# Position-dependent 7x7 attention: the two logits layers on four 64x64 parts of the array, positions as a matmul, one maximum call, filled three-tap slots

## The chip, the core and the metric

The kernel runs on one core of a Trainium2 chip. The time is that of one execution of the whole program on the device, in microseconds (us); the times below are medians over runs. The profile is one execution taken by the hardware profiler. Engine names are those of the profile: PE (matmul), PEld (its weight load), DVE (VectorE), ACT (ScalarE), POOL (GpSimd), SP (SyncE, which issues most DMAs here).

## The reference, cut to what matters

The program has two layers on a tensor of 4 images, 256 channels, 56x56. The change lies in the first. After a group norm, three 1x1 convolutions give `x1` and `x2` (32 channels) and `x3` (256 channels). For each of the 49 taps of a 7x7 window (borders reflected):

```python
sub2 = x1[:, :, None] - unfold_patches(x2)            # 32 channels
subp = p[:, :, None] - unfold_patches(p)              # 2 channels, positions only, the same for every image
y = relu(bn_eval(concat([sub2, subp])))               # 34 channels x 49 taps x 3136 places
y = relu(bn_eval(conv1x1(y, cw1)))                    # 34 -> 32   ("hidden")
wgt = softmax(conv1x1(y, cw2, cb2), axis=taps)        # 32 -> 32   ("logits")
out[:, :, s] = sum over taps of patch(x3)[:, :, s] * wgt[tap]    # 32 weights, each for 8 channels s
```

The second layer (attention with squared scores, a router that picks half of the tokens, a feed-forward on those) is not touched.

## The kernel before

**Tiling.** All is float32. An image is cut into 14 blocks of 4 rows (`RB`), 224 places each; 4 images give 56 blocks. The 128 partitions hold 4 taps x 32 channels. The 49 taps make 13 slots (`SLOTS`, L77): ten of 4 taps, and three, slots 10 to 12, of 3 taps, which use 96 partitions (`size`). A slot's patch is a shifted view into a ring of rows in SBUF, `ac` for `x2` and `xc` for `x3`, whose four partition groups were loaded with shifts of 0 to 3 columns; `aw` and `xw` serve the slots whose taps are neighbours downwards.

**A block's work.** `relation` (L488): `differ` subtracts on POOL into `y1`, `bend` does the first ReLU on ACT, `hidden` is the first matmul with `cw1`, a 128x128 matrix with four 32x32 blocks on its diagonal, `bend_more` the second ReLU on ACT (out of PSUM into `y2`), `logits` the matmul with `cw2`, of the same form, and `keep` copies the logits with their bias to `lg` on ACT. These four go by pairs of slots: a matmul of 400 columns (50 inner columns of 4 rows, 2 slots) for `hidden`, 448 for `logits`. `softmax` (L611) takes the maximum over slots on DVE, then over the four taps within the partitions by two matmuls with a rotation matrix (`turn`), subtracts, exponentiates, and sums. `values` (L690): 8 of the 13 products with `x3` on DVE (1792 elements each, weights copied to PSUM by `weights` first), 5 on POOL, and `add` sums each product over its taps into PSUM by four matmuls of 32 columns of the array (`same`), which run side by side.

**Positions.** What the two position channels add to `hidden` is the same for all inner columns of an inner block. `positions` (L247) works it out once; the inner columns get it as the bias `tb` of `bend_more`, one ACT instruction for each slot. The 3 columns at each side go a way of their own: `borders` (a matmul of 240 and one of 72 columns), `place_borders` (DVE, adds `near`), `bend_borders` (ACT). In the first and the last block of an image `load_pos` fetches the positions by DMA on ACT's queue, and `hidden` adds them by a second matmul for each pair of slots.

**Beside it.** `planes` (L298) makes `x1`, `x2`, `x3` of a following image in chunks of 8 rows, one chunk for each block, as 12 passes of 448 columns; its `x3` is taken out of PSUM by DVE. `statistics` makes the group norm's sums of an image, `ready` the layer norm of finished chunks of image 0, one in every second block's time from the eighth to the twentieth.

**Order.** Each engine's instructions stand in the order of the program (`InOrder`). The loop (L809) goes over steps, 14 (`ROUND`) for a block; `AT` (L94) gives each part its step and its rank within the step, counted from a block's own start. Blocks overlap: a block's `hidden` runs some 30 steps ahead of its products. Matmul outputs of `relation`, `planes`, `statistics` and `ready` share the PSUM pool `mm`: 4 buffers of one bank. Products share `prod`, 4 buffers in SBUF; a product takes the buffer that was given back first.

Of the kernel before, what the change touches and what calls it, by code (L numbers as in the profile page):

```python
# [7 lines left out]
F32 = mybir.dt.float32  # L8
# [7 lines left out]
P = 128  # L16
# [5 lines left out]
PAD = 3  # L22
# [24 lines left out]
    + ["b1", "b2", "cb2", "b3_0", "b3_1", "q_0", "q_1", "k_0", "k_1", "v_0", "v_1", "pb_0", "pb_1"]  # L47
# [11 lines left out]
def bn_affine(nc, pool, par, n, eps, tag):  # L59
# [12 lines left out]

ROW, COLUMN = 0, 1
# [10 lines left out]
HALVES = [(0, 10), (10, 13)]  # L84
INNER = W - 2 * PAD
# [9 lines left out]
    "load_relation": (-12, 4), "load_first": (23, 4), "load_values": (32, 5), "differ": (-5, 6),  # L95
    "bend": (-2, 9), "load_pos": (-1, 7), "hidden": (4, 5), "borders_0": (1, 5),
    "place_borders_0": (3, 9), "bend_borders_0": (6, 9), "borders_1": (3, 5),
    "place_borders_1": (7, 0), "bend_borders_1": (14, 3), "bend_more": (5, 5), "logits": (7, 1),
    "keep": (8, 7), "begin": (22, 1), "largest_0": (23, 3), "largest_1": (25, 6), "split": (27, 0),
    "join": (27, 7), "turned_0": (28, 7), "over_0": (29, 1), "turned_1": (29, 4), "over_1": (30, 1),  # L100
    "lower_0": (30, 1), "exp_0": (31, 0), "lower_1": (32, 5), "exp_1": (32, 8), "lower_2": (31, 9),
    "exp_2": (33, 0), "add_up_0": (33, 4), "add_up_1": (33, 5), "gather": (34, 1),
    "spread": (34, 1), "invert": (36, 1), "weights": (31, 5), "ours": (33, 0), "add_ours": (34, 0),
    "pools": (33, 6), "add_pools": (36, 9), "divide": (47, 1), "more": (51, 7), "store": (55, 3),
# [6 lines left out]
def conv_layer(ctx: ExitStack, tc: tile.TileContext, d, xs: bass.AP, ln0: bass.AP):  # L111
# [16 lines left out]
    bordersd = dram.tile([8, NS, 3 * FB4], F32, name="bordersd")  # L128
    insided = dram.tile([8, NS], F32, name="insided")
# [4 lines left out]
    )  # L134
    whole_image = lambda a, n: a[n].rearrange("(c p) f -> p c f", p=P)
# [21 lines left out]
    cw1p = const.tile([8, P], F32, name="cw1p")  # L157
# [3 lines left out]
    turn = const.tile([P, 2, P], F32, name="turn")  # L161
    nc.scalar.dma_start(turn, d["turn"])
# [18 lines left out]
    mm = ctx.enter_context(tc.tile_pool(name="mm", bufs=4, space=PSUM))  # L181
# [12 lines left out]
    def statistics(n):  # L194
# [13 lines left out]
        pm = mm.tile([P, 512], F32, tag="mm", name=f"pm{n}")  # L208
        te.matmul(pm[:, 0:2], gavg, mv[:, :, 0], start=True, stop=True)
# [7 lines left out]
        pv = mm.tile([P, 512], F32, tag="mm", name=f"pv{n}")  # L217
        te.matmul(pv[:, 0:2], gavg, dv, start=True, stop=True)
# [14 lines left out]

    tb = const.tile([P, NS], F32, name="tb")
    near = const.tile([P, 3, NS * RB * 2 * PAD], F32, name="near")
# [9 lines left out]
    def positions():  # L247

        pl = pp.tile([8 * NS, 2, 3 * FB4], F32, name="pl")
        ve.tensor_scalar(pl, loc[:, 0], pposs[:, 4:5], None, ALU.mult)  # L250
        yield
        ve.scalar_tensor_tensor(pl, loc[:, 1], pposs[:, 5:6], pl, ALU.mult, ALU.add)
        yield
        ve.tensor_scalar(pl, pl, pposs[:, 6:7], None, ALU.add)
        cen = pp.tile([8 * NS, 3 * FB4], F32, name="cen")
        ve.tensor_tensor(cen, pl[:, 0], pl[:, 1], ALU.subtract)
        yield
        se.activation(cen, cen, AF.Relu, bias=tp1, scale=sp1)
        inside = pp.tile([8 * NS, 1], F32, name="inside")
        ve.tensor_copy(inside, cen[:, FB4 + W // 2 : FB4 + W // 2 + 1])  # L260
        less = pp.tile([8 * NS, 3 * FB4], F32, name="less")
        ve.tensor_scalar(less, cen, inside, None, ALU.subtract)
        for j in range(2):
            r = slice(j * 4 * NS, (j + 1) * 4 * NS)
            nc.sync.dma_start(insided.rearrange("(g j) t -> j t g", j=2)[j], inside[r])
            nc.scalar.dma_start(bordersd.rearrange("(g j) t f -> j t g f", j=2)[j], cen[r])
            nc.sync.dma_start(posd.rearrange("(g j) t f -> j t g f", j=2)[j], less[r])
        at8 = pp.tile([8, NS], F32, name="at8")
        nc.sync.dma_start(at8, insided)
        edge = pp.tile([8, 3, NS, RB, 2, PAD], F32, name="edge")  # L270
        for b in range(3):
            for i in range(2):
                at = b * FB4 + i * (W - PAD)
                src = bordersd[:, :, at : at + 1]
                nc.scalar.dma_start(
                    edge[:, b, :, :, i],
                    bass.AP(
                        src.tensor, src.offset,
                        [list(src.ap[0]), list(src.ap[1]), [W, RB], [1, PAD]],
                    ),  # L280
                )
        for _ in range(10):
            yield
        pt = mm.tile([P, 512], F32, tag="mm", name="pinside")
        te.matmul(pt[:, :NS], cw1p, at8, start=True, stop=True)
        ve.tensor_scalar(tb, pt[:, :NS], s2, t2, ALU.mult, ALU.add)
        n = NS * RB * 2 * PAD
        for b in range(3):
            pt = mm.tile([P, 512], F32, tag="mm", name=f"pnear{b}")
            te.matmul(  # L290
                pt[:, :n], cw1p, edge[:, b].rearrange("p t h i w -> p (t h i w)"),
                start=True, stop=True,
            )
            ve.tensor_scalar(near[:, b], pt[:, :n], s2, t2, ALU.mult, ALU.add)
# [3 lines left out]
    def planes(n, q):  # L298
# [13 lines left out]
        pt = mm.tile([P, 512], F32, tag="mm", name=f"p12_{at}")  # L312
        for c in range(2):
            te.matmul(pt[: 2 * REL, :CH], w12[:, c], t[:, c], start=c == 0, stop=c == 1)
# [15 lines left out]
        for g in range(2):  # L330
            pt = mm.tile([P, 512], F32, tag="mm", name=f"p3_{at}_{g}")
            for c in range(2):
                te.matmul(
# [4 lines left out]
            ve.tensor_scalar(  # L338
                stag[:, g, own, PAD : PAD + W],
                pt[:, :CH].rearrange("p (h w) -> p h w", w=W),  # L340
                col(f"b3_{g}"), None, ALU.add,
# [40 lines left out]
    prod = ctx.enter_context(tc.tile_pool(name="prod", bufs=4))  # L382
# [10 lines left out]
    y1s = [yp.tile([P, NS, FB4], F32, name=f"y1_{i}", bufs=1) for i in range(2)]  # L393
    y2 = yp.tile([P, NS, FB4], F32, name="y2", bufs=1)
    xc = x3p.tile([P, SH, RING, WP], F32, name="xc", bufs=1)
    ac = ap.tile([P, 1, RING, WP], F32, name="ac", bufs=1)

# [38 lines left out]
    def patch(k, ring, w, t, which):  # L436
# [5 lines left out]
        return a[: taps * REL, which, r : r + RB, kj : kj + W]  # L442
# [34 lines left out]
    size = lambda t: SLOTS[t][3] * REL  # L477
    pairs = [(t, min(t + 2, NS)) for t in range(0, NS, 2)]

    def inner(y, t, e, pn):  # L480

        return view(y[:pn], t * FB4 + PAD, [[W, (e - t) * RB], [1, INNER]])

    def outer(y, t, e, pn):

        return view(y[:pn], t * FB4, [[W, (e - t) * RB], [W - PAD, 2], [1, PAD]])

    def relation(k):  # L488

        aw, a1 = held.pop(("a", k))  # L490
        border = {0: 0, H // RB - 1: 2}.get(blocks[k][1])
        y1 = y1s[k % 2]
        p1s, p2s = {}, {}

        def differ(i):

            a, z = GROUPS[i]
            m, pn = z - a, size(a)
# [3 lines left out]
                y1[:pn, a:z].rearrange("p t (h w) -> p t h w", w=W),  # L502
                a1[:pn].unsqueeze(1).to_broadcast([pn, m, RB, W]),
# [7 lines left out]
        def bend(i):  # L511
            a, z = GROUPS[i]
            se.activation(y1[: size(a), a:z], y1[: size(a), a:z], AF.Relu)

        def hidden(t, e):
            p1 = p1s[t] = mm.tile([P, 512], F32, tag="mm", name=f"p1_{k}_{t}")
            n = (e - t) * RB * INNER
            te.matmul(
                p1[:, :n], cw1[: size(t)], inner(y1, t, e, size(t)),
                start=True, stop=border is None, skip_group_check=True,  # L520
            )
            if border is not None:
                te.matmul(
                    p1[:, :n], cw1p, inner(held.pop(("pos", k, t)), 0, e - t, 8),
                    start=False, stop=True, skip_group_check=True,
                )

        def borders(i):

            t, e = HALVES[i]  # L530
            p1 = p1s["borders", i] = mm.tile([P, 512], F32, tag="mm", name=f"pb_{k}_{i}")
            te.matmul(
                p1[:, : (e - t) * RB * 2 * PAD], cw1[: size(t)], outer(y1, t, e, size(t)),
                start=True, stop=True,
            )

        def place_borders(i):

            t, e = HALVES[i]
            n = RB * 2 * PAD  # L540
            pn = size(t)
            be = p1s["placed", i] = yp.tile(
                [P, HALVES[0][1] * n], F32, tag="be", name=f"be_{k}_{i}", bufs=2
            )
            ve.scalar_tensor_tensor(
                be[:pn, : (e - t) * n], p1s.pop(("borders", i))[:pn, : (e - t) * n], s2[:pn],
                near[:pn, 1 if border is None else border, t * n : e * n],
                ALU.mult, ALU.add,
            )
# [1258 lines left out]
```

## Time and profile before

| | us |
|---|---|
| median of 3 runs (3821.7 to 3825.9) | 3825.31 |
| the profiled execution's own time | 3829.45 |
| its span | 3827.1 |
| first subtraction on POOL (`y<-a,ac`) | 76.4 |
| first `o<-acc,rz` (a block's end on DVE) | 172.2 |
| last `o<-acc,rz` | 1864.4 |

The first layer fills the span up to 1864 us, the second one the rest. Busy over the whole span: PE 91%, DVE 66%, ACT 52%, POOL 51%; the granted clock of PE was 0.954 on average and 1.00 in most blocks of the first layer. The `o<-acc,rz` rows, one for each block, cut the first layer into blocks, so that the distance of two of them is what one block costs. Of the 55 distances, 17 are 25.8 to 26.0 us, 15 are 30.4, four are 35.0, three are 27.4 to 27.8; ten lie between 31.0 and 38.8 around the end of an image, five between 36.3 and 56.8 where the statistics of an image are made, and the last is 17.1. Blocks of 30.4 have a chunk of `planes` in them, those of 35.0 also one of `ready`.

### The profile page before, as it was taken

The numbers are of one execution on the slowest core, as the hardware profiler recorded it, in microseconds if no ns is written. First come the engines' busy times: TensorE is split into PE (matmuls) and PEld (weight loads), VectorE is DVE, ScalarE is ACT, GpSimd is POOL, SyncE is SP. The second block draws the span as 40 slices with busy tenths as digits, with TensorE's granted clock in tenths as the row PEclk, the third lists the DMA queues.
The fourth block names the chain that finished last, engine by engine and source line by source line (L and its number), as shares of the span: only waits on it lengthen the run. The fifth ranks groups of instructions, "written<-read, shape, count | busy, mean of one in ns | idle before, by whom it ended". The sixth has DMA issues, their size and how long they took to land. (4 is left out here: it accounts for less than half of the span.)

```text
span 3827.1 us, 77232 instructions
## 1 busy us (share of the span) xinstructions
PE 3464.3 (91%) x30654; PEld 1469.0 (38%) x30654; DVE 2512.9 (66%) x3475; ACT 1991.4 (52%) x4181; POOL 1937.2 (51%) x1165
## 2 busy tenths in 40 slices
PE   3989998999979998999799989898899989889999
PEld 1333333333323333333243334333433344335666
DVE  2688888889778988999773457444754475434211
ACT  2767766777557765776235533444345424442111
POOL 1568887789768887998650026022512142110321
PEclk7999999999989999999899899998999999899999
DMA  3756656665566646655302210132012200231110
GB/s 97 161 134 145 138 133 157 141 136 105 131 143 141 138 91 136 128 117 108 99 2 50 57 46 7 41 83 60 10 29 73 64 19 12 60 93 40 55 51 27
DMA packets 328007, 330.99 MB, mean 86 GB/s; under 512 B 68651, under 2 KB 315407, under 8 KB 327647
## 3 DMA queue, kind: packets, MB, share of 16 engines
q1 hardware_dynamic: 309509, 289.68, 33.6%
q0 software_dynamic: 11408, 32.32, 2.7%
q10 hardware_dynamic: 6730, 4.05, 0.5%
q8 instruction: 241, 3.95, 0.4%
q14 instruction: 119, 0.97, 0.1%
HBM read 256.78 MB, written 68.68 MB: 85 GB/s over the span
## 5 line engine op out<-in xcount | busy, mean ns | idle before, releaser
L858 POOL TENSOR_TENSOR pr<-xc,lg 128x1792 f32<-128x1792 f32 x280 | 1034.9, 3705 | 279.0 <-ACT lg L858 102.2
L858 PE MATMUL acc<-pr,same 128*32 128x448 f32 (+1 forms) x5824 | 678.0, 558 | 71.0 <-DVE pr L858 57.0
L858 PE MATMUL p<-y,cw 128*128 128x400 f32 (+5 forms) x1568 | 681.9, 539 | 2.4 <-ACT y L858 1.5
L858 DVE TENSOR_TENSOR pr<-xc,exp 128x1792 f32<-128x1792 f32 x280 | 559.6, 1999 | 53.9 <-DMA xc<-x3d 30.2
L858 ACT ACTIVATE ph<-pg,unit 128x896 f32<-128x896 f32 x448 | 426.2, 1000 | 250.3 <-PE pg L858 249.5
L858 ACT ACTIVATE y<-p,tb,bn2s 128x200 f32<-128x200 f32 (+1 forms) x728 | 341.8, 519 | 226.3 <-PE p L858 222.1
L858 PEld LDWEIGHTS p<-y,cw 128*128 128x128 f32 (+1 forms) x1568 | 266.2, 191 | 399.7 <-issue 202.4
L858 POOL TENSOR_TENSOR phi<-ls 128x512 f32<-128x512 f32 (+1 forms) x200 | 242.9, 1215 | 264.0 <-PE accs L858 155.9
L858 DVE TENSOR_TENSOR phi<-pv,ls 128x1408 f32<-128x1408 f32 (+1 forms) x200 | 322.0, 1619 | 67.4 <-PE accs L858 48.6
L858 DVE TENSOR_TENSOR pr<-xw,exp 128x1792 f32<-128x1792 f32 x168 | 338.5, 2016 | 41.2 <-issue 16.0
L858 POOL DMA_DIRECT2D out<-tk x28 | 20.9, 746 | 647.9 <-ACT tk L858 599.5
L858 PE MATMUL pg<-qT,pairs 32*128 32x448 f32 x1792 | 303.9, 610 | 46.4 <-ACT ph L858 46.3
L858 POOL TENSOR_TENSOR y<-a,ac 128x896 f32<-128x896 f32 x168 | 277.7, 1654 | 126.7 <-DMA ac<-x3d 95.7
L858 PEld LDWEIGHTS acc<-pr,same 128*32 128x32 f32 (+1 forms) x5824 | 144.4, 110 | 429.9 <-issue 247.2
L858 POOL DMA_INDIRECT us<-rows,to x112 | 107.6, 961 | 320.7 <-DMA us<-rows,to 223.8
L858 ACT ACTIVATE ls<-pv 128x256 f32<-128x256 f32 (+1 forms) x200 | 77.3, 386 | 366.1 <-PE pv L858 333.7
L858 PE MATMUL accs<-phi,v 128*32 128x512 f32 (+1 forms) x1600 | 219.8, 613 | 38.2 <-POOL phi L858 27.9
L858 PE MATMUL pv<-wqkv,xn 128*32 128x256 f32 x3136 | 215.8, 390 | 42.4 <-DVE phi L858 22.7
L858 ACT ACTIVATE lg<-p,par 128x448 f32<-128x448 f32 x392 | 233.1, 595 | 4.6 <-PE p L858 4.6
L858 PE MATMUL acc<-ph,cf 128*32 128x448 f32 (+1 forms) x1792 | 229.8, 586 | 0.0
L858 ACT ACTIVATE lg<-lg 128x1120 f32<-128x1120 f32 x168 | 163.9, 1007 | 97.3 <-DVE lg L858 96.8
L858 DVE COPY av<-acc 128x448 f32<-128x448 f32 x56 | 35.0, 625 | 272.2 <-PE acc L858 272.1
(256 smaller groups left out, 5276.9 us busy)
## 6 DMA issues: line engine op xcount, KB each, us to landing
xw<-x3d SPq DMA_DIRECT2D x224, 248.0 KB
xq<-in_x SPq DMA_DIRECT2D x47, 448.0 KB
xc<-x3d SPq DMA_DIRECT2D x54, 248.0 KB
xc<-x3d SPq DMA_DIRECT2D x54, 247.0 KB
xc<-x3d SPq DMA_DIRECT2D x54, 246.0 KB
xc<-x3d SPq DMA_DIRECT2D x54, 245.0 KB
xr<-in_x SPq DMA_DIRECT2D x224, 56.0 KB
xs<-xr SPq DMA_DIRECT2D x224, 56.0 KB
```

The source lines that it names most:

```text
L858: return lambda *a, **k: self.tc.keep_in_program_order(of(*a, **k))
```

## The change

- `hidden` and `logits` use the array as four parts of 64 rows by 64 columns. `cw1` has nothing outside its diagonal blocks, so its upper left 64x64 serves taps 0 and 1 and its lower right 64x64 taps 2 and 3. Four slots make a batch (`BATCHES`, 3 of four slots and one of slot 12 alone): four matmuls of 448 columns, one for each part of the array, go to `p1[slot pair, tap half]`, and the tap halves lie in two PSUM banks. `logits` turns this back.
- Positions: `pos`, a constant tile of 13 slots, is a second set of four matmuls in every batch of every block (`cw1p`). It is reloaded by SP, batch by batch, where the next block's kind (first, inner, last of an image) differs. `tb`, `near`, `borders` and what belongs to them are gone.
- `bend_more` is one ACT instruction of 128x896 for a batch, `keep` one of 128x896, or two of 128x448 in the batch where slots 10 and 11 have 3 taps.
- The three slots of 3 taps get a fourth whose logit is -1e30 (`cb2_3`), so that all instructions have 128 partitions; the columns of the rings that this tap reads are set to 0 once.
- The maximum over slots is one `tensor_reduce` over 13 x 224 elements; that over taps is two transposes, a `tensor_reduce`, and eight matmuls of 32 columns of the array.
- `weights` copies two slots at a time. `planes` takes `x3` out of PSUM on ACT instead of DVE. The other matmuls of the layer are cut into quarters of 32 columns of the array (`by_quarters`).
- `mm` has 2 buffers of two banks, `prod` 5 buffers, `y1` one buffer instead of two. `AT` is new; `load_relation` moves from step -12 to -8, against a first `differ` at step -4 instead of -5.

```diff
-    mm = ctx.enter_context(tc.tile_pool(name="mm", bufs=4, space=PSUM))
+    mm = ctx.enter_context(tc.tile_pool(name="mm", bufs=2, space=PSUM))
...
+    matmul = lambda out, lhsT, rhs, start, stop: by_quarters(te, out, lhsT, rhs, start, stop)
...
-            ve.tensor_scalar(
+            se.activation(
                 stag[:, g, own, PAD : PAD + W],
                 pt[:, :CH].rearrange("p (h w) -> p h w", w=W),
-                col(f"b3_{g}"), None, ALU.add,
+                AF.Identity, bias=col(f"b3_{g}"),
             )
...
+    def batch(a, q, j):
+        if q < BATCHES - 1:
+            return a[:, 4 * q + 2 * j : 4 * q + 2 * j + 2]
+        return a[:, NS - 1, j * (FB4 // 2) : (j + 1) * (FB4 // 2)]
+    halves = [slice(i * HALF_P, (i + 1) * HALF_P) for i in range(2)]
+    width = lambda q: 2 * FB4 if q < BATCHES - 1 else FB4 // 2
...
-        def hidden(t, e):
-            p1 = p1s[t] = mm.tile([P, 512], F32, tag="mm", name=f"p1_{k}_{t}")
-            n = (e - t) * RB * INNER
-            te.matmul(
-                p1[:, :n], cw1[: size(t)], inner(y1, t, e, size(t)),
-                start=True, stop=border is None, skip_group_check=True,
-            )
+        def hidden(q):
+            n = width(q)
+            p1 = p1s[q] = mm.tile([P, 2, 512], F32, tag="mm", name=f"p1_{k}_{q}")
+            for w, of in ((cw1, y1), (cw1p, pos)):
+                for i, taps in enumerate(halves):
+                    for j, to in enumerate(halves):
+                        te.matmul(
+                            p1[to, i, :n], w[taps, taps], batch(of, q, j)[taps],
+                            start=of is y1, stop=of is pos, skip_group_check=True,
+                        )
+            if after != kind:
+                load_pos(4 * q, min(4 * q + 4, NS), after, sy)
...
-        def bend_more(t, e):
-            p1 = p1s.pop(t)
-            n = RB * INNER
-            for a in range(t, e):
-                pn = size(a)
-                se.activation(
-                    inner(y2, a, a + 1, pn),
-                    p1[:pn, (a - t) * n : (a - t + 1) * n].rearrange("p (h w) -> p h w", w=INNER),
-                    AF.Relu, bias=tb[:pn, a : a + 1], scale=s2[:pn],
-                )
+        def bend_more(q):
+            n = width(q)
+            y2 = y2s[q] = yp.tile([P, 2, 2 * FB4], F32, tag="y2", name=f"y2_{k}_{q}")
+            se.activation(y2[:, :, :n], p1s.pop(q)[:, :, :n], AF.Relu, bias=t2, scale=s2)
+        def logits(q):
+            n = width(q)
+            p2 = p2s[q] = mm.tile([P, 2, 512], F32, tag="mm", name=f"p2_{k}_{q}")
+            y2 = y2s.pop(q)
+            for j, part in enumerate(halves):
+                for i, taps in enumerate(halves):
+                    te.matmul(
+                        p2[taps, j, :n], cw2[part, part], y2[part, i, :n],
+                        start=True, stop=True, skip_group_check=True,
+                    )
...
-        def begin():
-            se.activation(z[:, :, :FB4], lg[:, 0:2], AF.Identity)
-        def largest(*parts):
-            for t, i, n in parts:
-                m = z[: size(t), i : i + n, :FB4]
-                ve.tensor_tensor(m, lg[: size(t), t : t + n], m, ALU.max)
...
+        def largest():
+            ve.tensor_reduce(mx, lg.rearrange("p t f -> p f t"), AX.X, ALU.max)
+        def turned():
+            for i in range(2):
+                te.transpose(
+                    z[:TB, 0, i * P : (i + 1) * P], mx[:, i * TB : (i + 1) * TB], ident
+                )
+        def over_turned():
+            ve.tensor_reduce(
+                most, z[:TB, 0, :].rearrange("p (i g c) -> p i c g", i=2, g=4), AX.X, ALU.max
+            )
+        def turned_back():
+            for i in range(2):
+                for j in range(4):
+                    te.matmul(
+                        z[j * REL : (j + 1) * REL, 1, i * TB : (i + 1) * TB], most[:, i],
+                        ident[:TB, :TB], start=True, stop=True, skip_group_check=True,
+                    )
```

## The prediction

> **What bounds the kernel now.** I read the granted clock first (1.00 in the blocks below), then the busy time by windows that run from one `o` row to the next, one block each, then the groups by shape inside five plain blocks (1634.64 to 1764.26 us), then the timeline of PE for what one pass costs. Windows (length, then busy us of PE, PEld, DVE, ACT, POOL; clock; DMA):
>
> ```profile
> 897.54:923.44 25.90, 25.84 (x170) 9.83 (x168) 25.63 (x25) 18.95 (x41) 25.73 (x11) 1.00 0.52 109
> 652.32:682.73 30.41, 30.41 (x181) 11.63 (x181) 27.08 (x28) 24.24 (x63) 26.49 (x11) 1.00 0.64 152
> 682.73:717.69 34.96, 33.62 (x189) 13.03 (x189) 31.14 (x34) 27.35 (x62) 27.23 (x12) 1.00 0.63 137
> 949.34:981.09 31.75, 31.75 (x178) 11.24 (x170) 25.89 (x26) 18.95 (x41) 25.13 (x11) 1.00 0.60 119
> ```
>
> A plain block (first line) has three engines full at once: PE, DVE and POOL. With `planes` (second) or position matmuls (fourth) PE alone is full; with `ready` too (third) PE has 33.62 of 34.96. So less work on PE and DVE helps wherever a block is longer than 25.9, and POOL, whose work stays, holds a plain block where it is.
>
> Groups in the five plain blocks:
>
> ```profile
> L858 POOL TENSOR_TENSOR pr<-xc,lg 128x1792 f32<-128x1792 f32 x16 | 59.2, 3716 | 0.7 <-ACT lg L858 0.6
> L858 POOL TENSOR_TENSOR y<-a,ac 128x896 f32<-128x896 f32 x5 | 9.8, 1962 | 0.0
> L858 DVE TENSOR_TENSOR z<-lg,z 128x448 f32<-128x448 f32 x20 | 12.5, 623 | 0.3
> L858 ACT ACTIVATE y<-p,tb,bn2s 128x200 f32<-128x200 f32 x51 | 23.7, 518 | 13.7 <-PE p L858 13.6
> ```
>
> The timeline of PE (start, us), in the first layer and in the second:
>
> ```profile
> 1025.41 0.96 PE L858 MATMUL acc<-pr,same 128*32 128x448 f32 x8
> 1026.30 1.73 PE L858 MATMUL p<-y,cw 128*128 128x400 f32 x4
> 1027.96 1.71 PE L858 MATMUL acc<-pr,same 128*32 128x448 f32 x16
> 1029.60 1.73 PE L858 MATMUL p<-y,cw 128*128 128x400 f32 x4
> ...
> 2173.80 0.94 PE L858 MATMUL pu<-qT,gram 128*32 128x448 f32 x8
> 2174.66 1.03 PE L858 MATMUL pg<-qT,pairs 32*128 32x448 f32 x8
> 2175.62 0.96 PE L858 MATMUL acc<-ph,cf 128*32 128x448 f32 x8
> ```
>
> Each matmul shows as two instructions. Eight more `acc` lengthen the row by 0.75 us, so a pass of 448 columns costs 0.375 us, and four parts of the array share one pass. `pg` shows this for four parts by rows (1.03 for 8). Changing the form costs extra: `acc` to `p` 0.89 and 1.64 instead of 0.75 and 1.50 (+0.14), `p` to `acc` 1.66 instead of 1.41 (+0.25); into and out of `pg` 0.86 and 0.96 instead of 0.75 (+0.11, +0.21).
>
> **PE.** 64x64 parts are not in the trace. The nearest rows are `acc` (four by columns) and `pg` (four by rows), both at once; I take four at once. The bounds are that, and two at a time (twice the passes). A plain block before: `hidden` 6 pairs x 0.667 + 0.33, borders 0.52, `logits` 6.5 x 0.75, together 9.7; 8 changes of form and back x 0.39 = 3.1. After: three batches x (2 + 2 + 2) x 0.375 = 6.75 and the last batch 0.56, 7.3; 7 changes x 0.32 = 2.2. Rotation (4 passes of 224, 0.75) against transposes and 4 passes of 112 (0.5 to 1.2, I take 0.9). Sum: 25.84 - 9.7 - 3.1 - 0.75 + 7.3 + 2.2 + 0.9 = 22.7. `planes` adds 12 x 0.375 = 4.5 as before: 27.2; `ready` 3.0: 30.2. Quarters instead of 128x128 cost nothing by the `acc` rows (same 0.375).
>
> A rule against this: the Trainium skill, "TensorE: Matmul & The Clock Gate", section "Measured speedup vs the span model", gives 3.07x, not 4x, for four row tiles. By it my estimate of a four-part pass is 0.49 us, plain PE 25.0, and blocks with `planes` would gain next to nothing (sum -55 instead of -92); the `pg` row shows no such loss.
>
> **DVE.** Plain block, work alone: maxima 4 x 0.66 + 0.66 + 0.30, `join` and two after the rotations 1.08, `place_borders` 0.58, together 5.2, go. Rows of the second layer (112 partitions): `w<-uw` reduces 1024 elements in 1.21 us and `per<-hit` 420 in 0.59, so 1.03 ns for one; 2912 elements make 3.1 and 256 make 0.4. DVE has 25.9 - 5.2 + 3.5 = 24.2. The new read steps 896 bytes between slots; no row has that: bounds 3.1 and 6.2 (twice); I take 3.1, as the products read shifted rows at 1.1 ns. In `planes` blocks 1.4 more goes to ACT.
>
> **ACT.** Gone in a plain block: 13 x 0.52, 6 x 0.62 + 0.44, borders 0.66, `begin` and `split` 0.9, copies 8 x 0.35 = 15.3. New: `bend_more` 3 x 1.0 + 0.45 (`ph<-pg` 128x896 takes 1.0), `keep` 2 x 1.0 + 2 x 0.62 + 0.44, copies 4 x 0.55 = 9.3. ACT falls from 18.95 to 13.0: never the bound. But 2 buffers of `mm` put it between PE's matmuls. After `hidden` PE has about 1.2 to 2 us of `add` and sums before the `logits` that need the drain; drain and handover take 1.0 + 0.3, so plain blocks wait little, and 2.9 us of PE are free there. With `planes`, its second `x3` matmul waits until ACT, behind an exponential (0.75) and two `bend` (0.76 each), has drained the first, and its first one waits for `bend_more`: I take 1.0 a block (27.2 becomes about 28.4 with 0.2 for slower starts), bounds 0 and 7: eight matmul groups at 0.9, the mean of `pg` waiting for `ph` in the waits (46.3 us, 52 times).
>
> **POOL** has 5 x 3.72 + 6.5 + 1.16 = 26.2 by durations, 25.7 back to back; 96 or 128 partitions cost the same (3.7 both). A plain block stays 25.9; what is late next there is POOL.
>
> **Queues.** SP loses nothing and gets 8 `pos` DMAs at each of 11 changes of kind, 0.45 each, 3.6 us of a block in which its 24 DMAs take 11; behind them stand `ac` and `xc` loads with steps to spare. ACT's queue loses 48 loads. `load_relation` has 4 steps (7.4 us) instead of 7 to the first `differ`; on SP it moves behind `xw` and `xr` (8 issues, 3.6 us); its five first DMAs take 2.2 us to issue, and at 70.85 to 76.42 the subtraction began 0.7 us after the eighth: covered; if SP is late, POOL pays, 0 to 1.7 a block. In the opening ACT waits for `posd` as it did for `bordersd` (until 44 us), then drains four `x3` itself: +1.5 (bounds -4 and +5). `prod` with 5 buffers and `y1` with one: nothing; DVE's order of reuse asks only for sums done 3 us earlier.
>
> **Sum over the 55 distances.** 15 blocks of 30.4 become 28.5: -28 (0 to -42). Four of 35.0 lose 2.5: -10 (0 to -18). Ten at the image ends: seven border blocks x 5.85 (31.75 - 25.90) of position matmuls go, and a little of the rest that PE stretched: -45 (-25 to -77, all that is over 25.9); loads of `xc` that the waits show there (85.8 us in 6 waits of POOL) stay. Five with statistics: -10 (0 to -20), DVE being shorter. 20 plain: 0. Start +1.5. Together -92: 3829.45 - 92 = 3737; the median shown is 4 below the profiled execution: 3733. By the bounds this case spans 3664 to 3805.
>
> **Rivals.**
> A. Slower: PE and ACT hand two buffers to and fro, and PE waits s us in every block. Plain blocks have 3.2 us spare on PE, `planes` blocks the same against 30.4. For: `pg` waits 0.9 for a drain of the same size, 8 times 0.9 is 7. Against: between most pairs stand 1.5 us of other matmuls. At s = 5 plain blocks cost 1.8 more (20), `planes` and `ready` 1.8 (19), image ends 1.8 (10) less 45, statistics 1.8 (5): 54 x 1.8 - 45 = +52, 3877. It decides from s = 4.0.
> B. Slower: the parts run two at a time. Passes cost 7.3 more; plain 30.0, all 54 up by 4.1, less 45: +176, 4001. Against: `acc` and `pg`.
> C. Faster, less: the `planes` blocks are paced by ACT's drains and keep 30.4; only image ends and statistics gain: -55, 3770. For: its three outputs share the two buffers.
> D. `tensor_reduce` costs 6.2: DVE 27.3, plain blocks +1.4 x 20 = +28: -64, 3761. Four times (12.4) would give 33.5 a block and a loss of some 200.
>
> **How the numbers follow.** Likeliest 0.55, C 0.15, D 0.08 (0.06 faster, 0.02 slower), A 0.14, B 0.06, no net change by a mixture 0.02. Faster 0.55 + 0.15 + 0.06 less 0.01 that ends within 0.2% = 0.75; same 0.03; slower 0.22. 0.2%, 8 us, is about what a measurement tells from no change. 3675 to 3850 holds C, D, nearly all of the likeliest and the milder half of A, and leaves out B, D's worst and A's upper half.
>
> **What would show it.** Right: `p1` and `p2` rows of 64*64 at eight in about 1.0 us; plain distances of 25.8 with PE near 23 busy; `planes` distances of 28 to 29; image-end distances mostly under 33; the maximum's row near 3.2 us. Wrong: PE idle before `p` rows with ACT as releaser over 3 us a block (A), 64*64 passes of 0.75 (B), POOL idle on `ac` in plain blocks, a maximum over 5 us (D).

## The result, and the profile after

| | before | after |
|---|---|---|
| median of 12 runs, us | 3823.03 | 3829.35 |
| lowest and highest, us | 3818.9, 3831.2 | 3818.1, 3839.1 |
| span of the profiled execution, us | 3827.1 | 3827.3 |
| mean granted clock of PE | 0.954 | 0.936 |
| last `o<-acc,rz`, us | 1864.4 | 1868.3 |

After to before is 1.0016, with a 95% interval of 1.0003 to 1.0028: a difference of 0.2%, about the least that a measurement of this kernel can tell. 3733 us and a gain of 92 us were predicted. PE has shed 6% of the span (91% to 85% busy), and nothing of it has come out at the end.

The distances between the 55 pairs of `o` rows say where it went. "Two cures" is the kernel of the fifth experiment below; it is shown here because it makes the table complete (what it subtracts is not the true maximum).

| us, change against before | predicted | after | after with `keep` early | with two cures |
|---|---|---|---|---|
| 15 blocks with `planes` (30.4 each) | -28 | **+39.4** | -43.4 | -43.4 |
| 4 with `planes` and `ready` | -10 | -6.3 | -10.2 | -13.6 |
| 10 at the image ends | -45 | -49.3 | -51.6 | -66.0 |
| 5 counted with the statistics | -10 | **+16.6** | +10.8 | +5.2 |
| 20 plain blocks | 0 | +7.1 | +6.1 | -12.5 |
| start and last distance | +1.5 | -3.7 | -8.8 | -7.1 |
| last `o` row | -92 | +3.9 | -97.0 | -137.4 |

(One of the five, in which image 3 begins, turns out to have no `st<-xq` row on DVE. It went from 36.5 to 32.5 us.)

Groups of the page of after:

```profile
L795 DVE TENSOR_REDUCE mx<-lg 128x224 f32<-128x2912 f32 x56 | 300.1, 5359 | 81.6 <-ACT lg L795 81.6
L795 PE MATMUL p<-xq,w 128*32 128x448 f32 x1040 | 156.0, 593 | 113.1 <-ACT lg L795 68.1
```

The maximum takes 5.36 us, not 3.1. And PE, whose nine largest kinds of wait before had none for `lg`, now waits 68.1 us for it ahead of `p<-xq`, which is `p12`, the first matmul of `planes`.

Windows of after (length, then busy us of PE, PEld, DVE, ACT, POOL; clock; DMA): two plain blocks, one with `planes`, and the block in which image 1 begins, with statistics.

```profile
1639.58:1666.25 26.67, 23.82 (x256) 7.53 (x254) 26.32 (x17) 14.90 (x22) 25.77 (x11) 0.94 0.53 108
1666.25:1692.52 26.27, 22.25 (x256) 7.26 (x253) 26.27 (x17) 14.83 (x22) 25.82 (x11) 1.00 0.71 138
1148.24:1182.23 33.99, 29.90 (x292) 9.00 (x292) 26.62 (x15) 20.71 (x41) 25.97 (x11) 0.90 0.52 120
604.24:668.01 63.77, 29.07 (x272) 8.36 (x264) 39.64 (x36) 19.64 (x28) 33.03 (x13) 0.73 0.69 148
```

In the second plain block DVE is full from end to end, and PE has 4 us to spare at full clock (22.25 us). In the `planes` block no engine is full: PE is busy for 29.90 of 33.99 us, at a mean clock of 0.90. That clock comes from a stop. The timelines of PE and ACT in the next `planes` block (start, us, idle time before and what ended it):

```profile
1202.85 0.96 PE L795 MATMUL acc<-pr,same 128*32 128x448 f32 x8
1207.32 2.46 PE L795 MATMUL p<-xq,w 128*32 128x448 f32 x6 [3.51 <-ACT lg L795]
1208.83 0.96 PE L795 MATMUL acc<-pr,same 128*32 128x448 f32 x2
1209.57 0.96 PE L795 MATMUL p<-xq,w 128*32 128x448 f32 x2
1209.58 3.91 PE L795 MATMUL acc<-pr,same 128*32 128x448 f32 x14
1213.42 0.98 PE L795 MATMUL p<-y,cw 64*64 64x448 f32 x8
1214.22 0.93 PE L795 MATMUL p<-pos,cw1p 64*64 64x448 f32 x8
1214.97 0.37 PE L795 MATMUL p<-y,cw 64*64 64x112 f32 x8
```

```profile
1202.95 0.95 ACT L795 ACTIVATE y<-y 128x896 f32<-128x896 f32 x1 [2.14 <-POOL y L795]
1203.81 1.40 ACT L795 ACTIVATE xq<-xq,sh,rs 128x448 f32<-128x448 f32 x2
1205.11 1.12 ACT L795 ACTIVATE lg<-lg 128x1120 f32<-128x1120 f32 x1
1206.13 1.14 ACT L795 ACTIVATE lg<-p,par 128x448 f32<-128x448 f32 x2
```

`p12` needs an `mm` buffer. One of the two holds `hidden`'s batch 3, the other the logits of batch 2, which were finished by 1200.6. They are copied out by `keep` (`lg<-p`) only at 1206.13, because on ACT that copy stands behind a `bend` that waits 2.14 us for POOL, behind `planes`' own two normalisations, and behind an exponential. PE stands still for 3.51 us. Then every pass takes twice as long:

```profile
1199.60:1203.80 4.20, 4.15 (x52) 1.18 (x48) 4.20 (x4) 1.99 (x2) 4.20 (x3) 1.00 0.41 103
1207.32:1213.40 6.08, 6.08 (x24) 1.33 (x24) 2.12 (x2) 2.83 (x5) 3.94 (x2) 0.51 0.24 53
1213.40:1216.30 2.90, 2.83 (x34) 0.98 (x32) 0.00 (x1) 1.08 (x2) 2.90 (x2) 1.00 0.00 0
```

The clock granted was 1.00 before the stop, 0.51 in the 6.08 us after it, and 1.00 again from then on. The Trainium skill, "TensorE: Matmul & The Clock Gate", section "What's actually happening", says that an idle window of some 3.4 us halves the clock until a window of that length has been busy. This trace agrees on the halving, after 3.51 us idle, but its half clock lasted 6.08 us. A stop shorter than that window was enough in the first of the plain blocks above:

```profile
1649.38 2.43 PE L795 MATMUL acc<-pr,same 128*32 128x448 f32 x16 [2.42 <-DVE pr L795]
```

After these 2.42 us the granted clock was 0.51 from 1650.2 to 1653.7 us, which is the 0.94 of that block. There PE had the time to spare.

In the `planes` block the last sums of `acc` come late, and DVE, in whose queue the next maximum and the next products stand behind `o`, waits with them. DVE's waits of after, whole span:

```profile
DVE o L795 <- PE acc L795: 103.6, 26, 6.5
DVE mx L795 <- ACT lg L795: 81.6, 19, 75.9
DVE st L795 <- DMA xq<-in_x: 58.3, 8, 20.8
```

### The profile page after: what moved, and what is told of

The parts are those of the page before. It is cut to its first block, busy times and chain, and to the rows that moved or that the text cites. A ratio compares the mean times of both kernels' runs of the same rounds, so it can differ in the third digit from the quotient of the medians.

```text
span 3827.3 us, 86925 instructions
## 1 busy us (share of the span) xinstructions
PE 3260.6 (85%) x36238; PEld 1290.1 (34%) x36238; DVE 2503.2 (65%) x2909; ACT 1804.6 (47%) x3173; POOL 1944.3 (51%) x1168
## 5 line engine op out<-in xcount | busy, mean ns | idle before, releaser
L795 PE MATMUL acc<-pr,same 128*32 128x448 f32 x5824 | 727.9, 579 | 153.8 <-DVE pr L795 140.2
L795 DVE TENSOR_TENSOR pr<-xc,exp 128x1792 f32<-128x1792 f32 x280 | 561.7, 2007 | 22.1 <-ACT exp L795 13.4
L795 PE MATMUL p<-y,cw 64*64 64x448 f32 (+1 forms) x3584 | 387.6, 504 | 40.4 <-DVE lt L795 23.9
L795 DVE TENSOR_REDUCE mx<-lg 128x224 f32<-128x2912 f32 x56 | 300.1, 5359 | 81.6 <-ACT lg L795 81.6
L795 PEld LDWEIGHTS acc<-pr,same 128*32 128x32 f32 x5824 | 175.3, 113 | 475.7 <-DVE pr L795 212.2
L795 POOL TENSOR_TENSOR y<-a,ac 128x896 f32<-128x896 f32 x168 | 276.5, 1660 | 24.1 <-DMA a<-a1d 14.3
L795 ACT ACTIVATE y<-p,bn2t,bn2s 128x896 f32<-128x896 f32 x224 | 213.5, 953 | 142.0 <-PE p L795 141.9
L795 ACT ACTIVATE exp<-lg 128x448 f32<-128x448 f32 x224 | 122.2, 545 | 280.2 <-DVE pr L795 279.7
L795 PE MATMUL p<-xq,w 128*32 128x448 f32 x1040 | 156.0, 593 | 113.1 <-ACT lg L795 68.1
L795 PE MATMUL accs<-phi,v 128*32 128x512 f32 (+1 forms) x1600 | 219.8, 614 | 38.1 <-POOL phi L795 27.9
L795 ACT ACTIVATE lg<-p,par 128x896 f32<-128x896 f32 x280 | 200.5, 736 | 48.2 <-PE p L795 47.6
```

The source lines that it names most:

```text
L795: return lambda *a, **k: self.tc.keep_in_program_order(of(*a, **k))
```

## The experiments

Two theories were set against each other. **H**: two `mm` buffers and a late `keep` stop PE in the `planes` blocks. **M**: the strided maximum makes DVE the bound, and PE's waits lie beside it. All ratios are to the kernel before, run on the same chip.

### `keep` one step earlier

```diff
-    "bend": (0, 9), "hidden": (3, 2), "bend_more": (4, 8), "logits": (5, 3), "keep": (7, 3),
+    "bend": (0, 9), "hidden": (3, 2), "bend_more": (4, 8), "logits": (5, 3), "keep": (6, 8),
```

> Against 3829.4 us of the changed kernel. One edit: `keep` is entered one step earlier, so that on ACT the copy of batch 2's logits stands ahead of `planes`' two normalisations, of a `bend` and of an exponential. Theory H (two `mm` buffers: the late `keep` holds the buffer that `p12` needs, PE stands still for 3.5 us, runs at half clock after it, and `acc` and DVE's `o` come late): the wait of `p<-xq` for `lg` falls from 68.1 us in all to under 20, the fifteen `planes` blocks go from 33.0 to some 30 us between two `o`, and the kernel takes 45 us less, some 3785 us. Theory M (the strided maximum of 5.36 us makes DVE the bound everywhere, PE's waits are hidden): the wait goes and the time stays within 8 us of 3829. Either way the plain blocks stay at 26.5 us.

Measured: 3729.8 us, ratio 0.9751 (0.9729 to 0.9772). The group of `p12`, and DVE's wait for `acc`, in this kernel:

```profile
L795 PE MATMUL p<-xq,w 128*32 128x448 f32 x1040 | 137.8, 554 | 50.8 <-ACT xq L795 49.6 <-ACT lg L795 1.1
```

```profile
DVE o L795 <- PE acc L795: 26.4, 25, 3.4
```

The wait for `lg` has gone from 68.1 to 1.1 us, DVE's for `acc` from 103.6 to 26.4. Two `planes` blocks of this kernel in windows:

```profile
1081.15:1108.55 27.40, 26.57 (x296) 8.79 (x292) 26.39 (x15) 20.69 (x40) 25.80 (x11) 1.00 0.64 152
1108.55:1135.95 27.40, 26.57 (x296) 8.79 (x292) 26.37 (x15) 20.69 (x40) 25.82 (x11) 1.00 0.66 156
```

27.40 us at a clock of 1.00, against 33.99 at 0.90. Of the 6.6 us, 3.3 are PE's busy time (29.90 to 26.57, the half clock) and 3.3 its idle time (4.09 to 0.83). Over all fifteen blocks the mean fell by 5.5 us (33.03 to 27.51). H holds, and at twice the expected size: the expectation named the half clock, but its 45 us are 3 us for each of the fifteen blocks, about the stop alone. The plain blocks are where they were (26.47 on average, 26.52 in after). The edit moves the other work on ACT along, so this run alone does not tell the held buffer from ACT's order.

### The maximum read in order

```diff
-            ve.tensor_reduce(mx, lg.rearrange("p t f -> p f t"), AX.X, ALU.max)
+            ve.tensor_reduce(
+                mx, lg.rearrange("p t f -> p (t f)").rearrange("p (f t) -> p f t", t=NS),
+                AX.X, ALU.max,
+            )
```

> Against 3829.4 us of the changed kernel. `largest` reads the 2912 logits of a partition in the order in which they lie, thirteen neighbours to a group, instead of thirteen logits 224 elements apart; what is subtracted is then another value that is the same for all slots of a position, no longer the true maximum. Theory M (the stride makes the maximum cost 5.36 us instead of 3.1, and DVE is the bound): the row of `mx` falls to 3.1 us, the plain blocks go from 26.5 to 25.8 us where POOL bounds them (20 times 0.7, 14 us), the fifteen `planes` blocks lose the same 2.3 us (34 us): some 3780 us. Theory H (the `planes` blocks are set by the handover of `mm`): the row falls as well, the plain blocks take 14 us less, the `planes` blocks stay at 33.0: some 3815 us. Should the row stay at 5.4 us, the stride is not its cause.

Measured: 3791.8 us, ratio 0.9915 (0.9898 to 0.9932).

```profile
L798 DVE TENSOR_REDUCE mx<-lg 128x224 f32<-128x2912 f32 x56 | 178.1, 3181 | 80.4 <-ACT lg L798 80.4
```

The same 2912 elements take 3.18 us in the order in which they lie and 5.36 with steps of 896 bytes: 1.09 against 1.84 ns each. The plain blocks fell by 14.5 us in all, to a mean of 25.8, which is POOL's time; the `planes` blocks did not fall (500.5 us for 495.5). That is H's pattern. The kernel still gained more than H's 15 us, because the image ends (15.4 us) and the statistics' blocks (8.2) gained too, which the expectation had left out.

### The maximum in pairs

```diff
-            ve.tensor_reduce(mx, lg.rearrange("p t f -> p f t"), AX.X, ALU.max)
+            m = smp.tile([P, 6, FB4], F32, tag="m6", name=f"m6_{k}", bufs=1)
+            ve.tensor_tensor(m, lg[:, 0:6], lg[:, 6:12], ALU.max)
+            ve.tensor_tensor(m[:, 0:3], m[:, 0:3], m[:, 3:6], ALU.max)
+            ve.tensor_tensor(mx, m[:, 0], m[:, 1], ALU.max)
+            ve.tensor_tensor(mx, mx, m[:, 2], ALU.max)
+            ve.tensor_tensor(mx, mx, lg[:, 12], ALU.max)
```

> Against 3829.4 us of the changed kernel. The same maximum as in the changed kernel, taken by five pairwise instructions (1344, 672, 224, 224 and 224 elements) instead of one reduction. At 1.03 ns an element and some 0.06 us each they take 3.1 us for 5.36. Theory M: as with the reading in order, some 3780 us. Theory H: plain blocks 14 us less in all, `planes` blocks unchanged, some 3815 us.

Measured: 4034.3 us, ratio 1.0554 (1.0534 to 1.0573). Both theories missed by over 200 us. DVE and then POOL in a plain block of this kernel (start, us):

```profile
1700.19 4.98 DVE L800 TENSOR_TENSOR m<-lg 128x1344 f32<-128x1344 f32 x1
1705.21 4.21 DVE L800 TENSOR_TENSOR m<-m 128x672 f32<-128x672 f32 x1
```

```profile
1700.05 8.64 POOL L800 TENSOR_TENSOR pr<-xc,lg 128x1792 f32<-128x1792 f32 x2
```

The spread of the first pair over the 56 blocks (ns, least, median, most):

```profile
L800 DVE TENSOR_TENSOR m<-lg x56: 1541/4415/12225, 99.6 to 2032.9; 128x1344 f32<-128x1344 f32 x56
```

The first pair takes 1.54 us at the least and 4.98 here: it starts just after one of POOL's products, and ends 1.4 us after that product's 3.7 us are over. POOL's two products then take 8.64 us instead of 7.4. The two engines go one after the other. The products of DVE do not suffer from it (2.00 us); they read one operand from PSUM, the pairs read both from SBUF. The Trainium skill, "SBUF — State Buffer", section "🔬 SBUF: two separate sides", states this: a DVE instruction with two SBUF inputs and a GpSimd instruction that reads SBUF exclude each other for their whole length. This run agrees (4.98 us for 1.54). It would also be what the copies of `weights` to PSUM buy, but no run took these away.

### Early `keep` and pairs

> Against 3829.4 us of the changed kernel. The early `keep` and the pairwise maximum together. If both causes hold and act in different places: plain blocks 25.8 us, `planes` blocks 28.5 us as the prediction had them, 15 times 4.5 and 20 times 0.7, some 80 us less, 3750 us, below the kernel before. Theory H alone: 3770 to 3785 us. Theory M alone: 3780 us, no less than with the pairwise maximum by itself.

The diffs are the two above. Measured: 4087.2 us, ratio 1.0681 (1.0656 to 1.0707). That is 337 us above the 3750 expected and 53 us more than the pairs alone: the blocks take 34.0 us (plain) and 33.8 (`planes`) for 32.9 and 33.2 there. The pairs stand behind POOL here too (the third, of 224 elements, takes 2.94 us on average for 0.39 at the least). So the run tells nothing of the two causes, and why the early `keep` costs time here is open.

### Early `keep` and the maximum in order

> Against 3729.8 us with the early `keep` alone. To it the maximum read in the order in which the logits lie (a value that is the same for all slots of a position, not the true maximum), 3.2 us for 5.4. Theory M' (once the handover is mended DVE, 26.4 us busy of 26.4 in the plain blocks, is the bound, and the whole shortfall of the maximum is still to be had): plain blocks 25.7 us on average as with the reading in order alone (22 times 0.7, 15 us), `planes` blocks from 27.4 to the 26.6 us that PE is busy in them (15 times 0.8, 12 us): some 3703 us. Rival: the `planes` blocks are now set by PE and stay at 27.4: some 3715 us. If the maximum cost nothing beyond DVE's slack: 3730 us.

Measured: 3691.5 us, ratio 0.9654 (0.9633 to 0.9675), 38 us less than the early `keep` alone and below all three of the expected times, which left out the image ends (-14.4) and the statistics' blocks (-5.6). Two plain blocks:

```profile
1430.75:1456.41 25.66, 22.46 (x260) 7.16 (x252) 24.12 (x16) 15.09 (x22) 25.66 (x11) 1.00 0.52 113
1456.41:1482.16 25.75, 22.48 (x260) 7.17 (x252) 24.14 (x17) 15.11 (x22) 25.75 (x11) 1.00 0.69 135
```

With the maximum at its assumed price DVE takes 24.1 us, PE 22.5, and POOL, full, sets 25.7. The `planes` blocks kept exactly 412.7 us in all, although DVE was busy 1.9 us less in them (24.48 us for 26.39): PE is the fullest engine there, with 26.59 of 27.40 us. So M, once the handover is mended, holds for the plain blocks, the image ends and the statistics' blocks, and its rival for the `planes` blocks.

### `keep` one step later

```diff
-    "keep": (7, 3),
+    "keep": (8, 7),
```

> Against 3829.4 us of the changed kernel. `keep` one step later than there (step 8, rank 7, where the kernel before has it), all else as in the changed kernel. Theory H: each step by which `keep` comes late holds a `mm` buffer longer; from the early entry to that of the changed kernel the fifteen `planes` blocks rose from 27.4 to 33 us. One step more must cost at least as much again in some blocks: above 3860 us, with the wait of `p<-xq` or `p<-y` for `lg` above the 68 us of the changed kernel. Rival: the gain of the early `keep` came from ACT's order as a whole (exponentials and `bend` later), not from the buffer: the time stays within 15 us of 3829 and the wait of PE for `lg` does not grow.

Measured: 3884.6 us, ratio 1.0154 (1.0131 to 1.0178). The time is as H has it, but the row that should have carried it is not. PE's waits for `lg` ahead of `p` fell from 68.7 to 48.4 us, and DVE's for `lg` rose from 81.6:

```profile
DVE mx L795 <- ACT lg L795: 172.9, 25, 79.6
```

A `keep` as late as this makes the logits late for the maximum itself. The run shows that the place of `keep` counts in both directions (100 us less a step earlier, 55 us more a step later). The added time goes with DVE's wait for the logits, so it is no support for the held buffer.

### `p12` one step later, `keep` left alone

```diff
         yield
+        if n or q > 1:
+            yield
         pt = mm.tile([P, 2, 512], F32, tag="mm", name=f"p12_{at}")[:, 0]
```

> Against 3829.4 us of the changed kernel. `keep` stays where the changed kernel has it; instead `planes` enters `p12` and all that follows it one step later, so that PE asks for the `mm` buffer after ACT has copied batch 2's logits, and ACT's exponentials, `bend` and normalisations keep their order. Theory H (it is the held buffer): the wait of `p<-xq` for `lg`, 68 us in all, falls below 20, the fifteen `planes` blocks fall from 33.0 to below 30 us, 3760 to 3785 us. Rival (the gain of the early `keep` came from ACT's order, whatever PE waited for): the blocks keep 32 to 34 us, 3815 us or more. A wait of `p3` for `p12`'s or its own drain may take a part of the gain.

Measured: 3813.0 us, ratio 0.9965 (0.9951 to 0.998). The `planes` blocks fell from 33.0 to 30.6 us, neither the 30 of H nor the 32 of its rival, and the time by 16 us only, to just under the rival's 3815: plain blocks (+7.5), those with `ready` (+4.9) and the start (+5.0) gave back half of those 36 us.

```profile
1140.50:1171.08 30.58, 27.36 (x300) 8.65 (x292) 26.71 (x15) 20.50 (x40) 25.66 (x11) 1.00 0.61 142
```

PE's busy time is 27.36 and its clock 1.00: the long stop and what it did to the clock are gone, although `keep`, the exponentials and `bend` stand on ACT as they did (the drains of `planes` itself moved with `p12`). The wait of `p12` for `lg` fell from 68.1 to 23.1 us, where H had below 20:

```profile
L797 PE MATMUL p<-xq,w 128*32 128x448 f32 x1040 | 144.8, 556 | 56.4 <-ACT xq L797 31.6 <-ACT lg L797 23.1 <-ACT y L797 1.0
```

Some 3.2 us of idle time are still there, in more and shorter waits:

```profile
1143.12 0.98 PE L797 MATMUL p<-y,cw 64*64 64x448 f32 x8 [0.58 <-ACT lg L797]
1148.48 0.98 PE L797 MATMUL p<-y,cw 64*64 64x448 f32 x8 [0.87 <-ACT stag L797]
1152.86 0.98 PE L797 MATMUL p<-y,cw 64*64 64x448 f32 x8 [0.62 <-ACT y L797]
1166.43 1.70 PE L797 MATMUL p<-xq,w 128*32 128x448 f32 x8 [0.86 <-ACT lg L797]
```

So the held buffer made the long stop: PE's request moved, and the stop went. The loss in a block has two parts that can be had apart: 2.5 us of half clock (29.90 to 27.36 us busy), which goes when no single wait is long, and some 3 us of waiting, nearly all of it ended by ACT. Only the early `keep` took out the second part, and with it ACT's order changes too; that this part is again the held buffers is likely, but no run shows it, and none gave `mm` a third buffer.

### The statistics a block later

```diff
-        first = max((n - 1) * (H // RB), NCH - 4)
+        first = max((n - 1) * (H // RB) + 1, NCH - 4)
```

> Against 3729.8 us with the early `keep` alone. To it the statistics and `planes` of images 2 and 3 one block later, so that the statistics no longer stand in the block in which an image begins. Theory Q (the 65.7 and 56.1 us between two `o` at the starts of images 1 and 2 are the statistics' loads and the new image's `xc` loads behind one another on SP's queue; the start of image 3, without statistics, takes 29.6 us): the two blocks fall to 30 to 45 us, the blocks after them rise from 27.9 to some 31, together 25 to 55 us less: 3675 to 3705 us. Rival: the image's first `xc` rows are late by themselves, and the statistics hide beside that wait: the two blocks keep some 50 us, the blocks after them rise by 3, and the time is 3720 to 3735 us.

The other rise of after is one block: the one in which image 1 begins went from 48.8 to 63.8 us. SP's queue there, in after (start, us to issue):

```profile
596.29 0.39 SPq L795 DMA_DIRECT2D xq<-in_x  x1
...
599.28 0.37 SPq L795 DMA_DIRECT2D xq<-in_x  x1
599.75 8.59 SPq L795 DMA_DIRECT2D xc<-x3d  x12
609.38 4.01 SPq L795 DMA_DIRECT2D xw<-x3d  x4
614.08 2.97 SPq L795 DMA_DIRECT2D xr<-in_x  x4
618.02 3.79 SPq L795 DMA_DIRECT2D xs<-xr  x4
621.91 5.15 SPq L795 DMA_DIRECT2D xq<-in_x  x3
```

The statistics' last chunks are asked for at 621.91, behind 24 other issues; DVE waits for one of them until 625.5 (20.7 us). In the kernel before, `load_values` was entered three steps later and SP issued two of these loads ahead of the twelve `xc`:

```profile
602.26 0.91 SPq L858 DMA_DIRECT2D xq<-in_x  x2
603.26 10.70 SPq L858 DMA_DIRECT2D xc<-x3d  x12
```

Measured (on top of the early `keep`): 3703.3 us, ratio 0.969 (0.9662 to 0.9717), 26 us less than the early `keep` alone. The two blocks fell from 65.7 and 56.1 to 35.7 and 37.6, those ahead of them by 5 each, but those behind rose from 27.9 to 44.1 and 42.2, not to 31. DVE's wait `st` for `xq` fell from 59.1 to 33.3 us. Q holds in sign, at the low end; a part of the wait moves along with the statistics.

### The statistics' loads on ACT's queue

```diff
-                ts.append(load(n, len(ts)))
+                ts.append(load(n, len(ts), se))
```

> Against 3729.8 us with the early `keep` alone. To it the statistics' later loads of the next image (four of seven chunks) issued on ACT's queue instead of SP's, where they stand behind twelve `xc` loads, four `xw`, four `xr` and a store. Theory Q: DVE's wait `st` for `xq` of 21 to 22 us at the two image starts falls below 6, the blocks of 65.7 and 56.1 us fall by some 15 to 20 us each: 3690 to 3705 us. Rival: the transfers and not their order on SP are late (the DMA share is 0.69 there): DVE's wait stays above 12 us, the time within 15 us of 3730, or above it where ACT, now waiting for a free buffer, keeps its exponentials back.

Measured: 3714.7 us, ratio 0.9707 (0.9686 to 0.9729), 15 us less than the early `keep` alone.

```profile
DVE st L795 <- DMA xq<-in_x: 26.0, 10, 7.0
```

The longest wait fell from 22.1 to 7.0 us (Q had below 6), and the two blocks by 17.0 and 15.0, as Q has it; the place on SP's queue made most of that wait. The blocks ahead of them rose by 5.3 and 7.6 us, so that two fifths of it came back, and the time missed Q's 3705 by 10 us. That the new `AT` put `load_values` in front is read from the two timelines; no run put it back alone.

### A true maximum through PSUM

```diff
-            ve.tensor_reduce(mx, lg.rearrange("p t f -> p f t"), AX.X, ALU.max)
+            m = exps.tile([P, 2, 256], F32, tag="exp", name=f"m_{k}")[:, :, :FB4]
+            ve.tensor_copy(m, lg[:, 0:2])
+            for t in range(2, NS - 1, 2):
+                ve.tensor_tensor(m, lg[:, t : t + 2], m, ALU.max)
+            ve.tensor_tensor(mx, lg[:, NS - 1], m[:, 0], ALU.max)
+            ve.tensor_tensor(mx, mx, m[:, 1], ALU.max)
```

> Against 3703.3 us with the early `keep` and the later statistics. To these the true maximum taken by eight instructions that keep their running maximum in PSUM, one copy of 448, five pairs of 448 with one operand in PSUM and two of 224. If a pair with an operand in PSUM goes at the 1.03 ns an element of the subtraction `lg<-lg,z`, and the 3.06 ns of the pairs with both operands in SBUF is DVE standing behind POOL's products, the eight take 3.7 us for 5.4; DVE then falls below POOL's 25.8 us, plain blocks go from 26.4 to 25.8 (22 times 0.6), `planes` blocks stay at 27.4: some 3685 us. Rival: PSUM does not help, the pairs take 3 ns an element there too: about 8 us, above 3800 us.

Measured: 3712.2 us, ratio 0.9711 (0.9692 to 0.9731), 9 us more than without it, with overlapping intervals (0.9662 to 0.9717 there): no gain, where 18 us were expected.

```profile
L800 DVE TENSOR_TENSOR m<-lg,m 128x448 f32<-128x448 f32 x280 | 175.9, 628 | 14.4 <-ACT lg L800 4.8
L800 DVE COPY m<-lg 128x448 f32<-128x448 f32 x56 | 35.1, 626 | 60.0 <-ACT lg L800 58.5
L800 DVE TENSOR_TENSOR mx<-lg,m 128x224 f32<-128x224 f32 x56 | 21.7, 388 | 12.2 <-ACT lg L800 6.4
```

With an operand in PSUM the pairs no longer stand behind POOL, but 6 x 0.63 + 2 x 0.39 make 4.5 us, not 3.7, and 0.8 us of DVE was won. The running maximum also takes one of the two buffers of `exps`, and ACT's idle time ahead of the copies of `weights` rose from 283.2 to 354.2 us, 206.3 of it ended by the maximum. That this ate the 0.8 us is likely and not shown.

The same with the statistics' loads on ACT's queue:

> Against the kernel with the early `keep`, the later statistics and the maximum through PSUM. To it the statistics' later loads on ACT's queue. With the statistics a block later DVE still waits 10.9 us for `xq` at the first of the two places; if the loads' place on SP makes that wait, 15 us less than without the edit in the four blocks around the two image starts, some 3670 us. Rival: with the statistics moved the loads have nothing in front of them, and ACT's issuing costs as much as it saves: within 6 us of the kernel without it.

Measured: 3709.2 us, ratio 0.9698 (0.9679 to 0.9717): 3 us less, inside the rival's bound and within the noise. The two cures of the statistics' loads do not add up.

The lowest median of a kernel that takes the true maximum is that with the early `keep` and the statistics a block later: 3703.3 us, 3% below the kernels before and after.

## Why the prediction was wrong

**Right.** The four 64x64 parts run at once: eight instructions, two passes, of `p<-pos,cw1p` take 0.75 us from their start to the next (1214.22 to 1214.97 in the first timeline of PE), 0.375 us a pass; rival B is out, and the weighed rule (0.49 us a pass) does not show here. PE in a plain block at full clock has 22.25 us (22.7 predicted), and DVE without the maximum's surplus 24.1 (24.2). POOL holds the plain blocks at 25.7 once DVE lets it. ACT has 14.9 us where 13.0 was said, of no consequence there. The image ends gave 49.3 us (45). With the early `keep` alone the last `o` row comes 97 us sooner, near the 92 predicted, but that is partly luck, as the steps do not come out one by one: `planes` blocks -43 for -28, statistics +11 for -10, start and last distance -9 for +1.5.

**Wrong, and decisive: the handover of `mm` in the `planes` blocks.** The step read "I take 1.0 a block (27.2 becomes about 28.4 with 0.2 for slower starts), bounds 0 and 7". It measured 6.6 in the block shown, near the upper bound, and 5.5 on average: 83 us over the fifteen blocks (495.5 us, 412.7 with the early `keep`). The sum did not carry its own bound either: 7 us make a block of 34.4 and 15 such blocks +60 us, but the range written for this step ends at 0. The place was wrong, too. The prediction looked at `x3`'s second matmul behind its own drain and the first behind `bend_more`. The stop came at `p12`, which needed the buffer of batch 2's logits, and `keep` stood on ACT behind a `bend` that waited for POOL, behind the normalisations that `p12` itself needs, and behind an exponential. And the price was that of a wait alone; the half clock behind a stop of 3.5 us cost as much again (3.3 and 3.3 us in the block shown). Rival A had this mechanism, but in every block with s from 4.0 upwards; it struck in the fifteen blocks with `planes`, and the plain blocks waited little, as the prediction said. Rival C, that these blocks keep 30.4 us, had the right blocks with the wrong size.

**Wrong in size: the maximum.** 5.36 us for 3.1, inside the bounds of 3.1 and 6.2 and above D's mark. DVE took 26.3 us of a plain block instead of 24.2 and became what is late there: 26.5 us for POOL's 25.7. In after that costs 7 us over the plain blocks against before; with the handover mended it is worth 38 us in all. "I take 3.1, as the products read shifted rows" compared runs of 56 neighbours with single elements 896 bytes apart. The Trainium skill, "SBUF — State Buffer", section "Door 1: The DMA port swizzle (why `[64,N]` ≈ `[32,N]`)", says that an access which crosses into another 16-byte line pays a penalty; the reading in order fits that, with 0.75 ns an element less for this instruction; that the lines are the reason is not shown, as only these two orders were run.

**Wrong in sign: the blocks with statistics.** "Five with statistics: -10, DVE being shorter" became +16.6, 15.0 of it in the block where image 1 begins. The part on the queues counted SP's time and the position loads, and followed `load_relation`; that `load_values` also moved ahead of the statistics' loads was not followed.

**The chances.** What came, the likeliest case's gain (97 us with the early `keep`) undone by A's mechanism in one class of blocks, is the mixture that had 0.02. Rival A was drawn up for all blocks alike; it needed a price for each class.

## What to carry to other kernels

When buffers are halved, list for every user of the pool which instruction of which engine gives the buffer back and what stands ahead of that instruction in its queue: here one entry of the table, a step earlier, was worth 100 us (3829 to 3730). Price a stop of PE of 3.5 us with the half clock behind it, and look for it in the class of blocks that has the extra user, not in the mean. Of an instruction with a new access pattern, look at how far apart neighbours lie in memory, and of an elementwise pair on DVE at whether both operands are in SBUF while POOL works.

## What was not expected of the hardware

- A reduction on DVE over elements 896 bytes apart goes at 1.84 ns an element, over neighbours at 1.09.
- A DVE pair with both operands in SBUF and a product on POOL exclude each other: 4.98 us for what takes 1.54 alone, and POOL's two products 8.64 for 7.4. A pair with one operand in PSUM does not wait, and costs 0.63 us for 448 elements.
- A stop of PE of 3.51 us was followed by 6.08 us at a clock of 0.51, which made as much of the loss as the stop; one of 2.42 us was followed by some 3.5 us at 0.51, and waits of 0.6 to 0.9 us left the clock at 1.00.
